# Last image of an attention and depthwise-conv kernel: division on chip for the last pair, four-part projection, x added by VectorE, and group averages on TensorE (first image too)

## The chip, the cores and the metric

The kernel runs on one core of a Trainium2 chip. Its time is device microseconds of one execution, the median of several. The engines are TensorE (PE in the profile; PEld is its weight load), VectorE (DVE), ScalarE (ACT), GpSimd (POOL) and SyncE (SP), which here only issues DMAs. Each engine takes its instructions in the order of the program and waits at the first one whose inputs or buffers are not ready. A DMA is issued from an engine's queue and waits there in the same way.

## The reference

x has shape (16, 384, 32, 32), all in fp32. Two layers, both with a residual and a group norm in front (32 groups of 12 channels):

```python
# _gn(v): (v - mean) / sqrt(var + 1e-5), per image, over a group's 12 channels and all pixels
def _L0_conv_ref(x, w_qkv, w_proj, b_proj):        # 8 heads of 48, n = 1024 pixels
    xt = x.reshape(b, c, n).transpose(0, 2, 1)
    qkv = einsum('bnc,oc->bno', xt, w_qkv)
    attn = softmax(einsum('bhnd,bhmd->bhnm', q, k) * SCALE)
    out = einsum('bhnm,bhmd->bhnd', attn, v)
    return einsum('bnc,oc->bno', out, w_proj) + b_proj
def _L1_conv_ref(x, weight):                       # depthwise, 7x7, padding 3
    w_sym = mean of the four rotations of weight
    return dwconv(x, w_sym)
x = x + _L0_conv_ref(_gn(x), ...)
x = x + _L1_conv_ref(_gn(x), weight)
```

## The kernel before

**Tiling.** An image is three tiles of 128 channels by 1024 pixels. The 8 heads are worked on in pairs, four pairs an image, 64 pairs in all (0 to 63); images are numbered 0 to 15. For a pair, attention runs over two halves of 512 queries and eight blocks of 128 keys. One step (`s_step`, `av_step`) is one half and one key block: two matmuls for the scores of the two heads, an exponential on ACT, two matmuls with v. Steps are issued in groups of four (GS), 16 groups an image; a group counts as r = 0, 4, 8 ... in the code, and is called group 0 to 15 here. V has a column of ones, so row 48 of a head's 64 accumulator rows holds the softmax sums. An fp32 matmul shows as two passes in the profile, each with its own weight load.

**Division and projection.** `take` copies a half of the accumulator to a tile `o` on ACT. `finish` then runs a chain: `sums_out` (L319, L320) writes the sum rows to DRAM and reads them back spread over partitions; `invert` takes the reciprocal (L326), writes it to DRAM (L328) and reads it back broadcast to 64 rows a head (L331); `divide` multiplies (L337). The fourth pair of an image is not projected by itself: its rows are copied by six DMAs (L342) into the unused rows of the three others, so that `proj_step` has three parts of 128 rows. `proj_step` ends with the bias on ACT (L360), and a DMA from POOL's queue that adds x in place (L361).

**Group norm.** `Stats.channels` takes channel statistics on VectorE (L184). `gather` sends them through DRAM so that one partition holds one group (L190, L192), `groups` aggregates them (L197), POOL works out scale and shift (L199 to L203), and two more DMAs through DRAM (L205, L209) bring them back to one row per channel. `apply` normalises a tile on a given engine (L215) or on ACT (L219).

**Depthwise conv.** For most tiles it is 49 multiply-adds on VectorE (`conv_tap`, L378), in place on the tile x1, and a DMA to the output from POOL's queue (L388). Of the last two images, tiles 2 and 1 go to TensorE instead: `conv_store` writes the normalised tile to DRAM (L450), `conv_load` reads shifted rows back (L457), four DMAs a load and two loads a half, `conv_on_pe` does a half of 16 rows with 112 passes (L478), and `conv_on_pe_end` adds the result from PSUM (L491). Its weight matrices are made by `conv_matrices` in group 4 and 6 of the last image.

**What sets the order.** The order on every engine is written out by a planner in the same Python code. `clock` stands for TensorE's time, `vclock` for VectorE's. After each group `catch_up` fills VectorE up to `clock`: a task of `later` whose due time has come, else the next conv tap of up to three active chains, each at an estimated cost (`us_tap`). `after(wait, cost, f)` sets a task due at `now() + wait`. The planner knows no lateness of the real engines: what it has put ahead of a task on VectorE stays ahead of it. After the last group a loop runs projection, conv halves (`half_on_pe`) and taps of the last two images until nothing is left. `check_vector` and `check_tensor` test all softmax sums for range at the end; a general version would run if they failed.

**Buffers.** PSUM has three two-bank tiles (`ps_s`, through `psum()`) for scores, q, k, v, projection and conv, and two one-bank tiles (`ps_o`) for attention. Tiles `o` have 6 buffers, x1 6, and `qk` 5, which the conv loads and one set of conv matrices share.

Of the kernel before, what the change touches and what calls it, by code (L numbers as in the profile page):

```python
# [10 lines left out]
F32 = mybir.dt.float32  # L11
# [10 lines left out]
SUM_LOW, SUM_HIGH = 1e-20, 1e20  # L22

# [17 lines left out]
def kernel(  # L41
# [7 lines left out]
    w_conv: bass.AP,  # L49
    out: bass.AP,  # L50
):

# [49 lines left out]
    def run(general):  # L102
        tag = "g" if general else "f"
        with ExitStack() as stack:
# [41 lines left out]
            load_x(0)  # L146
            wqk = wpool.tile([P, NK, 2, NK, P], F32, name="wqk")
# [11 lines left out]
            mhalf = wpool.tile([GROUPS, 1], F32, name="mhalf")  # L159
            nc.gpsimd.memset(mhalf, -0.5)  # L160
# [11 lines left out]
            wsh = wpool.tile([P, 2, 4, 2, KS], F32, name="wsh")  # L172

# [3 lines left out]
            class Stats:  # L177
# [16 lines left out]
                def groups(self):  # L194
# [6 lines left out]
                    nc.gpsimd.tensor_tensor(af[:, 0:1], ve, mhalf, ALU.pow)  # L201
# [8 lines left out]
                        self.sc, gr_d.rearrange("g e s -> (g e) s").rearrange("(k p) s -> p k s", p=P)  # L210
                    )
# [155 lines left out]

            def region(*ds):
                return [(slice(max(0, -d), H - max(0, d)), slice(max(0, d), H - max(0, -d))) for d in ds]
# [82 lines left out]
            def conv_load(b, k, h, a):  # L452
# [3 lines left out]
                for q in range(SH):  # L456
                    nc.sync.dma_start(  # L457
# [9 lines left out]
            def conv_on_pe(b, k, h):  # L467
                if h == 0:
                    pss[b, k] = psum(f"ps_conv_{b}_{k}")
# [4 lines left out]
                for n, (d0, dx) in enumerate(order):  # L474
                    _, (ox, ix) = region(0, dx)
# [115 lines left out]
            def us_tap(dy, dx):  # L591
                return ((H - abs(dy)) * (W - abs(dx)) + (130 if len(active) > 1 else 270)) / 940

            def tap():
# [3 lines left out]
                if not active:  # L598
                    return 0.0
                c = active.pop(0)  # L600
                b, k, n = c
                conv_tap(b, k, *TAPS[n])
                c[2] += 1
                took = us_tap(*TAPS[n])
# [40 lines left out]
            x1_made, lims = set(), []  # L645

            def project(b):
                nonlocal clock
                x1_made.add(b)
# [18 lines left out]
            def x1_chains(b, st):  # L668
                on_pe = [t for t in PE_TILES if t[0] == b]
                for k in range(NK - 1, -1, -1):  # L670
                    tail = b == B - 1
                    conv_begin(st, b, k, (nc.vector, nc.gpsimd, None)[k] if tail else nc.gpsimd)
                    if (b, k) in on_pe:
                        conv_store(b, k)
                        pe_conv.extend((b, k, h) for h in range(2))
                after(
                    1.0 if b == B - 1 else 6.0,
# [24 lines left out]
            def finish(u):  # L702
                sums_out(u)
                after(7.0, 0.3, lambda: finish2(u))
# [5 lines left out]
            def finish3(u):  # L710
# [4 lines left out]
                if u == U - 1:  # L715
                    after(0.5, 2.6, check_vector)
# [11 lines left out]
            st.gather()  # L728
            st.groups()
# [38 lines left out]
            def half_on_pe():  # L768
                nonlocal clock
                b, k, h = pe_conv.popleft()  # L770
                while (b, k, h, 1) not in shs:
                    loads(1)
                conv_on_pe(b, k, h)
# [91 lines left out]
```

## Time and profile before

| | |
|---|---|
| median of 3 runs | 3046.95 us (3046.26 to 3047.64) |
| the profiled execution's own time | 3048.38 us |
| its span, first to last instruction | 3046.5 us |
| TensorE clock granted, mean | 0.990 |
| DMA, mean over the span | 49 GB/s |

In a timeline, a row has the start in us, how long the row lasts (several instructions in a row are merged, "x36" counts them), the engine and the line, the operation, what it writes and reads, and in brackets the idle time of the engine before it with what ended it. "SPq" is a DMA that SP issues; the time is that of the issue. The start and the last 180 us are of interest here; the images between take 178 us each on TensorE.

How the share of busy time of the DMAs and TensorE's clock run in the tail, by stretches:

| us | PE busy | DVE busy | clock | DMA share, GB/s |
|---|---|---|---|---|
| 2840 to 2871 | 31.0 of 31 | 14.4 | 1.00 | 0.35, 101 |
| 2871 to 2881 | 2.1 of 10 | 9.7 | 0.82 | 0.90, 233 |
| 2881 to 2894 | 13.0 of 13 | 12.7 | 0.87 | 0.30, 71 |
| 2894 to 2921 | 0.4 of 27 | 26.4 | 0.57 | 0.23, 53 |
| 2921 to 2939 | 18.0 of 18 | 12.8 | 0.88 | 0.51, 96 |
| 2939 to 2973 | 34.0 of 34 | 5.3 | 1.00 | 0.55, 148 |
| 2973 to 3010 | 34.7 of 37 | 36.0 | 0.95 | 0.59, 149 |
| 3010 to 3046 | 13.9 of 36 | 24.9 | 0.75 | 0.08, 32 |

### The profile page before, as it was taken

Reading aid. Unit: us, or ns where it says so; the run is one execution under the profiler, and the core shown is the slowest. Engines: PE = TensorE matmul, PEld = TensorE weight load, DVE = VectorE, ACT = ScalarE, POOL = GpSimd, SP = SyncE. Lnnn points to the kernel's source line nnn. Section 1 sums busy time; section 2 is a strip of 40 time slices with the busy share of each in tenths; the row PEclk is TensorE's granted clock in tenths of the full one; section 3 lists DMA queues with packets and bytes.
Section 4 is the critical chain, followed back from the end, with each engine's and each line's share of the span. In section 5 each row is a group of like instructions: output and inputs, shape, how many; then the busy total and the mean of one; then the engine's idle time right before and its main releaser. Section 6 shows DMA issues by size and latency. Waiting matters only on the chain.

```text
span 3046.5 us, 30395 instructions
## 1 busy us (share of the span) xinstructions
PE 2955.0 (97%) x11586; PEld 1151.8 (38%) x11586; DVE 2606.9 (86%) x2532; ACT 1302.1 (43%) x1472; POOL 735.9 (24%) x440
## 2 busy tenths in 40 slices
PE   6999999999999999999999999999999999999866
PEld 2343343433434343343434334343433434343322
DVE  0001898996999999999999999999999999999757
ACT  1544435454443545434354543435354353535300
POOL 1021004020150604215060421506042150603310
PEclk9999999999999999999999999999999999999988
DMA  1113031021312112131211213121121312121343
GB/s 53 47 23 66 15 65 36 28 54 36 72 36 57 24 51 52 35 73 36 54 27 46 56 36 66 43 51 29 39 62 36 69 40 51 30 51 29 84 99 96
DMA packets 68252, 148.59 MB, mean 49 GB/s; under 512 B 31280, under 2 KB 33120, under 8 KB 66560
## 3 DMA queue, kind: packets, MB, share of 16 engines
q1 hardware_dynamic: 49280, 94.15, 12.6%
q0 software_dynamic: 18816, 52.40, 7.8%
q8 instruction: 93, 1.52, 0.2%
q14 instruction: 63, 0.52, 0.1%
HBM read 98.08 MB, written 29.54 MB: 42 GB/s over the span
## 4 chain that ended last, share of the span: by engine, by line
PE 93%; DVE 4%; issue 1%; DMA 1%; POOL 0%; SPq 0%; ACT 0%; POOLq 0%; DVEq 0%
PE ps_s L285 30%; PE acc L301 29%; PE ps_qk L234 17%; PE ps_proj L352 8%; PE ps_v L260 8%; DVE x L378 3%; PE ps_conv L478 1%; DMA x<-in_x 0%; DMA o<-o 0%; DMA wc<-in_w_conv 0%; POOL v L167 0%; DVE o L337 0%; DVE x L491 0%; DMA ch_x<-bs_x 0%; DMA sc_x<-gr_x 0%
## 5 line engine op out<-in xcount | busy, mean ns | idle before, releaser
L378 DVE SCALAR_TENSOR_TENSOR x<-xn,wsym,x 128x960 f32<-128x960 f32 (+9 forms) x2156 | 2382.0, 1175 | 19.0 <-POOL xn L215 15.8
L293 ACT ACTIVATE e<-ps_s 128x1024 f32<-128x1024 f32 x1024 | 967.1, 1030 | 394.4 <-PE ps_s L285 389.5
L285 PE MATMUL ps_s<-qk 48*128 48x512 f32 x4096 | 949.5, 603 | 2.2 <-ACT e L293 2.2
L301 PE MATMUL acc<-e,v 128*64 128x512 f32 x4096 | 937.7, 600 | 0.0
L285 PEld LDWEIGHTS ps_s<-qk 48*128 48x128 f32 x4096 | 373.3, 186 | 566.8 <-issue 430.6
L234 PE MATMUL ps_qk<-x,wqk 128*128 128x512 f32 x1152 | 507.6, 597 | 29.5 <-DVE x L215 29.5
L301 PEld LDWEIGHTS acc<-e,v 128*64 128x64 f32 x4096 | 272.0, 137 | 634.9 <-issue 563.2
L361 POOL DMA_DIRECT2D x<-in_x x48 | 42.3, 882 | 1488.1 <-ACT x L360 1483.1
L234 PEld LDWEIGHTS ps_qk<-x,wqk 128*128 128x128 f32 x1152 | 217.3, 191 | 312.5 <-issue 278.8
L199 POOL TENSOR_SCALAR ve_x<-mv_x 32x1 f32<-32x1 f32 x32 | 317.2, 9912 | 40.3 <-DVE mv_x L197 38.8
L241 ACT COPY qk<-ps_qk 128x1024 f32<-128x1024 f32 x96 | 97.2, 1012 | 465.6 <-PE ps_qk L234 465.6
L352 PE MATMUL ps_proj<-o,wp 128*128 128x512 f32 x576 | 253.6, 599 | 27.0 <-DMA o<-o 27.0
L260 PE MATMUL ps_v<-wv,x 128*128 128x384 f32 x768 | 254.5, 488 | 0.0
L184 DVE BATCH_NORM_STATS2 bs_x<-x 128x6 f32<-128x512 f32 x192 | 120.3, 681 | 109.6 <-DMA x<-in_x 92.2
L215 POOL TENSOR_SCALAR xn<-x,sc_x 128x1024 f32<-128x1024 f32 x46 | 195.1, 4248 | 40.1 <-DMA sc_x<-gr_x 40.0
L312 ACT COPY o<-acc 128x512 f32<-128x512 f32 x128 | 75.1, 587 | 296.7 <-PE acc L301 296.7
L260 PEld LDWEIGHTS ps_v<-wv,x 128*128 128x128 f32 x768 | 144.7, 190 | 113.6 <-issue 20.3
L326 DVE RECIPROCAL rec<-sums 128x16 f32<-128x16 f32 x64 | 16.0, 250 | 190.8 <-DMA sums<-sum 190.8
L352 PEld LDWEIGHTS ps_proj<-o,wp 128*128 128x128 f32 x576 | 109.0, 191 | 171.5 <-issue 167.9
L360 ACT ACTIVATE x<-ps_proj,bp 128x1024 f32<-128x1024 f32 x48 | 53.4, 1113 | 256.8 <-PE ps_proj L352 252.8
L269 ACT COPY v<-ps_v 128x384 f32<-128x384 f32 x128 | 55.1, 483 | 196.9 <-PE ps_v L260 196.9
L337 DVE TENSOR_TENSOR o<-o,inv 128x1024 f32<-128x1024 f32 x64 | 78.7, 1230 | 55.0 <-DMA inv<-inv 29.6
(48 smaller groups left out, 415.5 us busy)
## 6 DMA issues: line engine op xcount, KB each, us to landing
inv<-inv SPq DMA_DIRECT2D x128, 256.0 KB
x<-in_x SPq DMA_DIRECT2D x48, 512.0 KB
x<-in_x POOLq DMA_DIRECT2D x48, 512.0 KB, 5.5
out<-x POOLq DMA_DIRECT2D x48, 512.0 KB, 3.8
qk<-qk SPq DMA_DIRECT2D x96, 128.0 KB
sh<-xd SPq DMA_DIRECT2D x64, 160.0 KB
o<-o SPq DMA_DIRECT2D x96, 64.0 KB
sum<-o SPq DMA_DIRECT2D x128, 4.0 KB
```

The lines of the kernel that those rows point to most:

```text
L184: nc.vector.bn_stats(self.bs[:, k, 6 * h : 6 * h + 6], src[:, h * HALF : (h + 1) * HALF])
L199: nc.gpsimd.tensor_scalar(ve, mv[:, 1:2], EPS, None, ALU.add)
L215: engine.tensor_scalar(dst, src, self.sc[:, k, 0:1], self.sc[:, k, 1:2], ALU.mult, ALU.add)
L234: nc.tensor.matmul(ps[:, h, :], lhsT=wqk[:, k, s, t, :], rhs=xns[b][:, k, h * HALF : (h + 1) * HALF], start=(k == 0), stop=(k == NK - 1),)
L241: nc.scalar.copy(halves(qks[u][:, s, :]), ps)
L260: nc.tensor.matmul(ps[:, j, 0:C], lhsT=xns[b][:, k, t * P : (t + 1) * P], rhs=wv[:, k, :], start=(k == 0), stop=(k == NK - 1),)
L285: nc.tensor.matmul(ps[:, j, :], lhsT=qks[u][r, 1, i * P : (i + 1) * P], rhs=qks[u][r, 0, h * HALF : (h + 1) * HALF], start=True, stop=True,)
L293: nc.scalar.activation(es[n], ps, AF.Exp, scale=SCALE)
L301: nc.tensor.matmul(accs[u, h][64 * j : 64 * j + 64, :], lhsT=v_of(u, i, j), rhs=e[:, j, :], start=(i == 0), stop=(i == NT - 1),)
L337: nc.vector.tensor_tensor(os_[u], os_[u], invs.pop(u), ALU.mult)
L352: nc.tensor.matmul(ps[:, h, :], lhsT=wp[:, t, o * P : (o + 1) * P], rhs=os_[NP * b + t][:, h * HALF : (h + 1) * HALF], start=(t == 0), sto ...
L378: nc.vector.scalar_tensor_tensor(acc, xn1s[b, k].rearrange("p (h w) -> p h w", w=W)[:, iy, ix], wsym[:, k, dy + PAD, dx + PAD : dx + PAD + 1],
```

## The change

Two inputs come from the host: `masks`, seven 128x128 blocks that average over a group's 12 channels (the three diagonal blocks and the four neighbours that share a group) and an eighth block that copies a head's sum row to its 64 rows; and `w_proj_4`, projection weights in four parts, one for each pair as it lies in its `o` tile, with zero rows for the rest.

In the first image the group statistics no longer go through DRAM. In the last image the last pair is divided half by half: a mask matmul spreads the sums, VectorE takes the reciprocal of 128x512 from PSUM and multiplies. The projection has four parts and is split: parts 0 and 1 are issued ahead of the last attention half's last four v steps, parts 2 and 3 after them. x is loaded straight into the x1 tiles, and VectorE adds projection, bias and x. A conv half on TensorE is cut in two pieces of 56 passes; conv loads in the tail are issued from SP and ACT in turn; the engines that normalise the last image's three tiles change; and the planner charges 0.06 us more for a tap of the last two images.

```diff
+            masks_0 = opool.tile([P, N], F32, tag="o", name="masks_0")
+                nc.sync.dma_start(masks_0, masks.rearrange("p b c -> p (b c)"))
...
+                def groups_on_pe(self, masks):
+                    st = small.tile([P, NK, 2], F32, tag="st", name=f"st_{self.name}")
+                    for k in range(NK):
+                        nc.vector.bn_aggr(st[:, k, :], self.bs[:, k, :])
+                    ps = ps_o.tile([P, HALF], F32, tag="acc", name=f"ps_st_{self.name}")
+                    def average(c0, src):
+                        for mo in range(NK):
+                            blocks = [n for n, b in enumerate(MASK_BLOCKS) if b[1] == mo]
+                            for n in blocks:
+                                ki = MASK_BLOCKS[n][0]
+                                nc.tensor.matmul(
+                                    ps[:, c0 + mo : c0 + mo + 1],
+                                    lhsT=masks[:, n, :],
+                                    rhs=src[:, ki : ki + 1],
...
+                    nc.vector.tensor_copy(mean, st[:, :, 0])
+                    average(0, mean)
+                    nc.vector.tensor_tensor(d, mean, ps[:, 0:NK], ALU.subtract)
+                    nc.vector.tensor_tensor(d, d, d, ALU.mult)
+                    nc.vector.tensor_tensor(d, d, st[:, :, 1], ALU.add)
+                    average(NK, d)
+                    nc.vector.tensor_scalar(d, ps[:, NK : 2 * NK], EPS, None, ALU.add)
+                    nc.gpsimd.tensor_tensor(self.sc[:, :, 0], d, mhalf, ALU.pow)
+                    nc.vector.scalar_tensor_tensor(
+                        self.sc[:, :, 1], ps[:, 0:NK], -1.0, self.sc[:, :, 0], ALU.mult, ALU.mult
...
+            def divide_at_once(u, h):
+                half = os_[u][:, h * HALF : (h + 1) * HALF]
+                ps = ps_o.tile([P, HALF], F32, tag="acc", name=f"ps_sum_{u}_{h}")
+                nc.tensor.matmul(ps, lhsT=late["masks"][:, 7, :], rhs=half, start=True, stop=True)
+                inv = tpool.tile([P, N], F32, tag="t", name=f"inv_{u}_{h}")[:, 0:HALF]
+                nc.vector.reciprocal(inv, ps)
+                nc.vector.tensor_tensor(half, half, inv, ALU.mult)
...
+            def proj_part(b, o, ts):
+                if o not in pps:
+                    pps[o] = psum(f"ps_proj_{b}_{o}")
...
+            def residual(b, o):
+                nc.vector.scalar_tensor_tensor(
+                    halves(x1s[b, o]), pps.pop(o), bp[:, o : o + 1], halves(x1s[b, o]), ALU.add, ALU.add
...
-                    nc.sync.dma_start(
+                    (nc.scalar if late.get("tail") and q % 2 else nc.sync).dma_start(
...
-                return ((H - abs(dy)) * (W - abs(dx)) + (130 if len(active) > 1 else 270)) / 940
+                late_us = 0.06 if active[0][0] >= B - 2 else 0.0
+                return ((H - abs(dy)) * (W - abs(dx)) + (130 if len(active) > 1 else 270)) / 940 + late_us
...
-                    conv_begin(st, b, k, (nc.vector, nc.gpsimd, None)[k] if tail else nc.gpsimd)
+                    conv_begin(st, b, k, (nc.gpsimd, None, nc.vector)[k] if tail else nc.gpsimd)
...
-                after(7.0, 0.3, lambda: finish2(u))
+                if u < U - 1:
+                    after(7.0, 0.3, lambda: finish2(u))
...
-            st.gather()
-            st.groups()
+            st.groups_on_pe(masks_0.rearrange("p (b c) -> p b c", c=P))
...
+                if n0 == NS - 2 * GS:
+                    after(3.5, 4.2, lambda: None)
+                    divide_at_once(U - 1, 0)
+                if n0 == NS - GS:
+                    for o in range(NK):
+                        proj_part(B - 1, o, (0, 1))
+                    clock += 2 * US_PROJ
...
+                    if r == 8 * GS:
+                        w4 = w_proj_4.rearrange("(t p) c -> p t c", p=P)
+                        nc.sync.dma_start(wp, w4[:, 0:NK])
+                        nc.sync.dma_start(late["w3"], w4[:, NK])
...
+                    if r == 8 * GS:
+                        t = opool.tile([P, N], F32, tag="o", name="masks_1")
+                        nc.sync.dma_start(t, masks.rearrange("p b c -> p (b c)"))
+                    if r >= 9 * GS and (b, 0) not in x1s and all(c[0] > b - 2 for c in active):
+                        for k in range(NK):
+                            x1s[b, k] = rpool.tile([P, N], F32, tag="x1", name=f"x1_{b}_{k}")
+                            nc.gpsimd.dma_start(
+                                x1s[b, k], x[b, k * P : (k + 1) * P].rearrange("p h w -> p (h w)")
...
-            while later or proj or chains or active or pe_conv:
-                if proj and proj[0][0] <= clock + 1.0:
-                    project(proj.popleft()[1])
-                elif pe_conv and (B - 1 in x1_made or pe_conv[0][2] == 0):
+            late["tail"] = True
+            b = B - 1
+            divide_at_once(U - 1, 1)
+            for t in (NP - 2, NP - 1):
+                for o in range(NK):
+                    proj_part(b, o, (t,))
+            clock += US_PROJ * 4 / 3 + 1.0
+            st = Stats(f"x1_{b}")
+            for o in range(NK):
+                residual(b, o)
+                st.channels(x1s[b, o], o)
+            conv_piece()
+            st.groups_on_pe(late["masks"])
+            clock += 7.0
+            x1_chains(b, st)
+            vclock = clock
+            after(4.0, 2.6, check_vector)
+            while later or chains or active or pe_conv:
+                if pe_conv:
...
-                    half_on_pe()
+                    conv_piece()
```

`conv_piece` is `half_on_pe` for one of two parts of a half: seven of the fourteen shifts, four row groups each. `x1_chains` is called without waiting for the six DMAs and POOL's steps that `gather` and `groups` made.

## The prediction

> **What bounds the kernel now.** I read the page first, then the chain of waits, then the timelines of single engines at both ends of the span. Image numbers run from 0 to 15, pairs of heads from 0 to 63, so image 15 owns pairs 60 to 63.
>
> ```profile
> PE 2955.0 (97%) x11586; PEld 1151.8 (38%) x11586; DVE 2606.9 (86%) x2532; ACT 1302.1 (43%) x1472; POOL 735.9 (24%) x440
> PE 93%; DVE 4%; issue 1%; DMA 1%; POOL 0%; SPq 0%; ACT 0%; POOLq 0%; DVEq 0%
> ```
>
> TensorE is busy for 2955.0 of 3046.5 us, which leaves 91.5 us idle. The timelines place nearly all of it: 29.46 before the first matmul, 7.87 + 26.60 + 2.4 after the last attention step, 22.6 after the last matmul; that is 88.9. So the middle is closed to this change, and what it can give lies at the two ends.
>
> The head, from the timeline:
>
> ```profile
> 8.03 3.65 DVE L184 BATCH_NORM_STATS2 bs_x<-x 128x6 f32<-128x512 f32 x6
> 14.23 0.78 POOL L190 DMA_DIRECT2D ch_x<-bs_x  x1
> 19.18 0.79 DVE L197 BATCH_NORM_AGGREGATE mv_x<-gs_x 32x2 f32<-32x144 f32 x1 [7.50 <-DMA gs_x<-ch_x]
> 28.59 0.81 DVE L215 TENSOR_SCALAR x<-x,sc_x 128x1024 f32<-128x1024 f32 x1 [8.61 <-DMA sc_x<-gr_x]
> 29.46 23.20 PE L234 MATMUL ps_qk<-x,wqk 128*128 128x512 f32 x48 [29.46 <-DVE x L215]
> ```
>
> The channel statistics are done at 11.68, yet x is normalised at 28.59: the 17 us between are four small DMAs in a row and POOL's memsets ahead of them.
>
> The tail, TensorE:
>
> ```profile
> 2868.24 3.65 PE L301 MATMUL acc<-e,v 128*64 128x512 f32 x16
> ...
> 2880.74 13.36 PE L478 MATMUL ps_conv<-sh,mat 128*32 128x512 f32 x108 [7.87 <-DMA sh<-xd]
> 2920.71 17.95 PE L352 MATMUL ps_proj<-o,wp 128*128 128x512 f32 x36 [26.60 <-DMA o<-o]
> 2938.59 34.37 PE L478 MATMUL ps_conv<-sh,mat 128*32 128x512 f32 x336
> ```
>
> and VectorE, whose last tap ends the kernel (3027.47 + 8.14 = 3035.61; one output DMA and the end of the program take the other 10.9):
>
> ```profile
> 2856.55 1.23 DVE L337 TENSOR_TENSOR o<-o,inv 128x1024 f32<-128x1024 f32 x1 [19.22 <-issue]
> 2857.69 11.60 DVE L378 SCALAR_TENSOR_TENSOR x<-xn,wsym,x 128x928 f32<-128x928 f32 x11
> 2869.20 0.25 DVE L326 RECIPROCAL rec<-sums 128x16 f32<-128x16 f32 x1
> 2869.37 15.43 DVE L378 SCALAR_TENSOR_TENSOR x<-xn,wsym,x 128x1024 f32<-128x1024 f32 x13
> 2884.71 1.22 DVE L337 TENSOR_TENSOR o<-o,inv 128x1024 f32<-128x1024 f32 x1
> ...
> 2896.71 0.25 DVE L326 RECIPROCAL rec<-sums 128x16 f32<-128x16 f32 x1
> 2896.87 19.65 DVE L378 SCALAR_TENSOR_TENSOR x<-xn,wsym,x 128x928 f32<-128x928 f32 x16
> 2916.43 1.22 DVE L337 TENSOR_TENSOR o<-o,inv 128x1024 f32<-128x1024 f32 x1
> ...
> 2964.20 0.82 DVE L215 TENSOR_SCALAR xn<-x,sc_x 128x1024 f32<-128x1024 f32 x1 [12.00 <-DMA sc_x<-gr_x]
> 2973.10 0.15 DVE L756 TENSOR_REDUCE good<-ps_again 1x1 f32<-1x2 f32 x1 [8.08 <-PE ps_again L754]
> ```
>
> The three divides are those of pairs 61, 62 and 63. Pair 63's attention ended at 2871.9 but was divided at 2916.43, because its reciprocal and its multiply each stood behind conv taps in VectorE's strict order. VectorE runs late, by the planner's clock some 25 us: pair 62's reciprocal is due about when group 11 ends (2843) and ran at 2869.20. The cause:
>
> ```profile
> 2799.00 38.42 POOL L199 TENSOR_SCALAR ve_x<-mv_x 32x1 f32<-32x1 f32 x1 [12.98 <-DVE mv_x L197]
> 2847.26 1.50 SPq L450 DMA_DIRECT2D xd<-xn  x2
> 2848.81 0.45 SPq L328 DMA_DIRECT2D inv<-rec  x1
> ```
>
> POOL's tiny operation (0.23 us in an idle stretch) is held until the taps stop at 2837.33; SP's store of image 14 waits for POOL; pair 61's inverse waits behind that store; VectorE stands 19.22 us for it. The change touches none of this, so the lateness stays, and it decides how much of the tail can be won. VectorE's idle time from 2856.55 to 3035.61 is 2.62 + 3.67 + 3.75 + 3.51 + 12.00 + 8.08 = 33.6 us, its work 145.4.
>
> **The change, part by part** (times on the old trace's clock).
>
> *Head.* Four DMAs and a [32]-row aggregation go. Added: a 512 KB load ahead of wqk on SP, three aggregations, a copy, two rounds of 7 fp32 matmuls (14 passes each, with one weight load per pass), three small VectorE operations between the rounds, one after, POOL's power, one VectorE operation. Steps: 11.7 end of statistics; 0.5 for the wc load sharing the DMAs (x moved at 400 GB/s, so 512 KB is 1.3 us, the upper end); aggregation 0.79 for 144 elements against 0.15 for a one-element operation gives 0.2 each, 0.6; copy 0.15; first round 14 x 0.34 (the weight load of a cold start) = 4.8; three operations 0.7 with hand-overs; second round 3.8 (between 14 x 0.34 and the warm 14 x 0.19); 0.25; POOL 0.57 + 0.2 (its memsets end at 14.3, before this); 0.25. Sum 23.5 against 28.59: 5.1 won. In the old head the first six passes run at 0.86 instead of 0.43, 2.5 us; some of it may be gone after the small matmuls: 0.4. **Taken: 5.5.** One-column passes are not in the trace: by ps_again's two (0.19 together) the 28 cost 2.7 and the gain would be 11, where wqk's landing stops it (the DMAs fall silent at about 16.5); by full 512-column warm passes (0.43) they cost 12 and it is 1.
>
> *Weights and masks on SP in group 8.* Three more DMAs, 1.3 MB, issued behind the blocked store, from 2852.5. At the 194 GB/s of that stretch 6.8 us, at the head's 400 GB/s 3.3, and about 1.5 to issue: masks are there at 2857 to 2861, and the first mask matmul is due at 2861.05. Queued behind them on SP are the conv loads of groups 10, 12 and 14 and pair 62's sums, needed at 2869.2 and before landed early enough. Taken: nothing; if the cover is gone each us stops TensorE, which has 20 us before VectorE reaches that half.
>
> *Loop end on TensorE.* One mask matmul 0.87 and 12 projection matmuls at 0.87 (a step's six take 5.2) before the last attention half: attention ends at 2883.2 instead of 2871.9. Projection over four pairs is 24 matmuls, 20.8 us instead of 15.65.
>
> *VectorE's queue.* From pair 61's divide (2856.55): 11 taps and pair 62's reciprocal to 2869.4, as before; 11 taps to 2882.6; first half's reciprocal and multiply; 2 taps and pair 62's divide to 2890.5; by the planner 13 more taps (the last group is 10.6 longer), to 2906; then the second half's reciprocal and multiply, to 2910.4. A 128x512 reciprocal is not in the trace. From 128x16 at 0.25 against 0.15 for one element: 6.7 ns an element, 3.6 + 0.15, **3.7 us taken**; lower end a 512-element statistics pass, 0.64; upper 32 x 0.25 = 8.0. Multiply 0.62.
>
> The Trainium skill ("VectorE: DVE Perf Modes", First, the fixed hardware budget) says that Reciprocal is an iterative divide with a repeat count of 8. At the 0.96 GHz of its Specifications, an estimate of 8 cycles for each of 512 elements is 4.3 us; the sum would end 1.2 us later.
>
> So pair 63 is divided 7 us earlier than before, not 40: its DRAM round trip goes, the taps ahead of it stay. TensorE does t=2 after 2890.5, idles to 2910.4, and runs t=3 in 7.7 (six passes at 0.86, six at 0.43).
>
> *Residual.* ACT's bias and POOL's accumulating DMA (1.11 + 5.5 landing) give way to 3 VectorE operations of 1.22 from PSUM. x is loaded early, after image 13's stores at 2870; 1.5 MB beside 1.3 MB of conv loads at 230 GB/s lands by 2887, needed at 2914. The statistics end at 2922. The first conv piece (56 passes, 5.7) stands ahead of the averages on TensorE until 2924; the averages then take two rounds of 3.5 plus 2 of small operations: 2933, against 2964.20 before.
>
> *Sum for VectorE.* Work: 145.4 - 0.25 - 1.14 - 0.79 + 2 x 4.32 + 3 x 1.22 + 1.5 (small ones) = 157.0. Taps: image 15's chain alone took 59.1 for 49 (1.206); three chains together 30 in 31.9 (1.063). 46 taps now run as two chains; the gain is 0 to 6.6, 5 taken: 152.0. Idle: 3.9 (for t=3), 9.5 (averages), 2 (POOL normalises tile 0 in 1.73, held while taps run, released when VectorE waits for it), 2 (check), 1: 18.4. End 2856.55 + 152.0 + 18.4 = 3027.0 against 3035.6: **8.6 won**.
>
> *Conv on TensorE* covers little now: 15 pieces at 5.8 from 2931.7, one wait of about 6 for loads queued behind the two stores of image 15, gives 3025 against 3023.9 before; VectorE's add after it ends level with the taps. Loads issued on ACT too: 302 to 1581 ns an issue before, so at most 0.5 us a load off SP; taken at nothing, ACT has one normalisation left.
>
> The Trainium skill ("DMA: Bandwidth & Descriptors", Issuing engines are not separate DMA queues) speaks against more: a second issuing engine saves issue time only. With the stretches at 1.05 share and 227 to 233 GB/s here, that would leave the 6 us wait whole.
>
> **Total** 5.5 + 8.6 = 14.1. The profiled span, 3046.5, is 0.45 below the shown median (its own run took 3048.38), so 3046.95 - 14.1 = **3033**.
>
> **Rivals.** *TensorE's conv becomes the bound* (chance 0.20). Before, one conv half ran in the wait for pair 63; now PSUM is held by the projection and all eight run after it. At 6.0 a piece (444 passes in 47.48) and two waits of 5 more the end is 3034: tail 1.5 won, **3040**. For it: 7.87 and 1.84 us waits for conv loads; against: loads run at 230 GB/s, 5.7 us a half, where TensorE takes 11.4. *Late VectorE recovers* (0.12): no stall at 19.22 with the shifted order, head at its good end: 9 + 15, **3023**. *Slower* (0.06): the same conv loads as a lasting bound. If each half waits 3 us and more for its rows, as DMAs from two queues and outputs meet, the seven halves after the first give 21 us: 3053; it decides from 2.0 us a half on, and the DMA share of 0.55 to 0.59 there is against it. *No effect* (0.03): masks late in the head, averages as slow as the DMAs, about 3046. The forecast has 0.59.
>
> The forecast alone spans 3027 to 3039; with the others and both ends of the unknown costs, 3022 to 3043. A measurement tells about 0.2% (6 us) from no change: faster by more 0.90, within 0.04, slower 0.06.
>
> **What would show it.** Right: first qk matmul near 24; a 128x512 reciprocal near 3.7; the second one starting 20 us or more after attention ends; projection t=3 waiting on that multiply; a gap of some 9 us on VectorE at the averages; last tap and last conv add within 3 us of each other. Wrong: TensorE waiting at the mask matmul; conv matmuls waiting for rows at most pieces; a last-half reciprocal with no taps ahead.

## The result, and the profile after

| | before | after |
|---|---|---|
| median of 4 runs, us | 3046.61 (3045.91 to 3047.64) | 3022.47 (3021.12 to 3024.64) |
| span of the profiled execution, us | 3046.5 | 3020.0 |
| TensorE clock granted, mean | 0.990 | 0.994 |

The change made the kernel faster: ratio 0.9921, 95% interval 0.9904 to 0.9938, 24.1 us in the medians. The forecast was 14.1 us and 3033, with a range of 3022 to 3043: the sign is right, the gain is 10 us larger than forecast, and the time lies 0.5 us inside the range. The forecast's own span, 3027 to 3039, misses it by 4.5 us.

The page of after, busy times and the shares of the chain of waits:

```profile
PE 2970.3 (98%) x11658; PEld 1166.2 (39%) x11658; DVE 2616.1 (87%) x2553; ACT 1298.7 (43%) x1469; POOL 728.3 (24%) x426
PE 90%; DVE 5%; issue 3%; POOL 1%; DMA 1%; ACT 0%; POOLq 0%; SPq 0%; DVEq 0%
```

TensorE has 15 us more to do (a fourth projection part, the mask matmuls) and idles 49.7 us instead of 91.5. So the gain, but for a place in the loop shown below, is idle time of TensorE at the two ends, and for the tail it is VectorE that decides how much.

*Head*, timeline of TensorE:

```profile
14.41 3.15 PE L236 MATMUL ps_st_x<-mn_x,masks 128*128 128x1 f32 x14 [14.41 <-DVE mn_x L245]
18.20 3.15 PE L236 MATMUL ps_st_x<-d_x,masks 128*128 128x1 f32 x14 [0.64 <-DVE d_x L250]
23.69 6.50 PE L280 MATMUL ps_qk<-x,wqk 128*128 128x512 f32 x11 [2.34 <-DVE x L261]
```

The first qk matmul stands at 23.69 instead of 29.46. Each round of 14 one-column passes takes 3.15 us, 0.225 a pass. Of the qk passes that follow four take the long 0.86 instead of six, so after image 0's first qk the kernel is 6.6 us ahead. In before, image 0's projection also waits 0.37 us for a row copy; in after it doesn't, and from there the kernel is 7.0 us ahead. The profile's clock shows 1.00 for all these rows, yet the long passes take as long as those at 0.50 in the tail (0.86), and so do the rounds (3.14 us at 0.50 in run e8, 1.72 at 1.00). That TensorE ran at half clock here is worked out from these times; the clock's row doesn't show it.

*A place in the loop that the change doesn't touch.* In group 10 of image 2 TensorE waits 2.22 us for an exponential, in both kernels. Before:

```profile
512.28 2.08 PE L285 MATMUL ps_s<-qk 48*128 48x512 f32 x4 [2.22 <-ACT e L293]
514.29 5.91 PE L301 MATMUL acc<-e,v 128*64 128x512 f32 x16
```

and after:

```profile
505.29 1.13 PE L331 MATMUL ps_s<-qk 48*128 48x512 f32 x4 [2.22 <-ACT e L339]
506.35 3.65 PE L347 MATMUL acc<-e,v 128*64 128x512 f32 x16
```

The same 20 passes take 7.92 us before and 4.71 after: in the profiled execution of before the granted clock fell to 0.50 there, in that of after it stayed at 1.00. That is 3.2 of the 26.5 us between the two spans. It is no effect of the change, as the twelve further traces show below.

*Tail*, VectorE:

```profile
2846.16 1.22 DVE L383 TENSOR_TENSOR o<-o,inv 128x1024 f32<-128x1024 f32 x1 [18.85 <-ACT e L339]
...
2894.01 3.35 DVE L420 RECIPROCAL inv<-ps_sum 128x512 f32<-128x512 f32 x1
2897.46 0.69 DVE L421 TENSOR_TENSOR o<-o,inv 128x512 f32<-128x512 f32 x1
2900.32 1.28 DVE L440 SCALAR_TENSOR_TENSOR x<-ps_proj,bp,x 128x1024 f32<-128x1024 f32 x1 [2.17 <-PE ps_proj L431]
...
2913.33 0.16 DVE L248 TENSOR_TENSOR d_x<-mn_x,ps_st_x 128x3 f32<-128x3 f32 x1 [4.03 <-PE ps_st_x L236]
...
3008.17 1.22 DVE L570 TENSOR_TENSOR x<-ps_conv,x 128x1024 f32<-128x1024 f32 x1
```

and TensorE:

```profile
2898.20 7.53 PE L431 MATMUL ps_proj<-o,mat 128*128 128x512 f32 x10 [10.94 <-DVE o L421]
2905.66 5.98 PE L557 MATMUL ps_conv<-sh,mat 128*32 128x512 f32 x56
2911.57 1.72 PE L236 MATMUL ps_st_x<-mn_x,masks 128*128 128x1 f32 x14
2913.94 2.71 PE L236 MATMUL ps_st_x<-d_x,masks 128*128 128x1 f32 x14 [0.65 <-DVE d_x L250]
2916.58 42.51 PE L557 MATMUL ps_conv<-sh,mat 128*32 128x464 f32 x388
```

Pair 61's divide (the first line) still stands 18.85 us, as it did before (19.22). From its start to VectorE's last instruction it is 163.2 us (2846.16 to 3009.39), before 179.1: **15.8 us won in the tail**. The named waits in that stretch are 2.17 and 0.81 for the projection's fourth part, 4.03, 2.80 and 1.01 in the averages, 10.8 together, against 33.6 before. TensorE runs its conv from 2916.58 to 3005.48 without once waiting for a row. Its clock fell to 0.50 once more during the second round of averages (2.71 us for 14 passes where the first took 1.72) and was back at 1.00 by 2922; no wait since 2898.20 had been longer than 0.65 us. That is about 1 us of VectorE's 2.80.

So 7.0 (head) + 3.2 (clock) + 15.8 (tail) + 0.5 (the rest) make the 26.5 us between the spans.

### The profile page after: what moved, and what is told of

The parts are those of the page before. It is cut to its first block, busy times and chain, and to the rows that moved or that the text cites. A ratio compares the mean times of both kernels' runs of the same rounds, so it can differ in the third digit from the quotient of the medians.

```text
span 3020.0 us, 30559 instructions
## 1 busy us (share of the span) xinstructions
PE 2970.3 (98%) x11658; PEld 1166.2 (39%) x11658; DVE 2616.1 (87%) x2553; ACT 1298.7 (43%) x1469; POOL 728.3 (24%) x426
## 4 chain that ended last, share of the span: by engine, by line
PE 90%; DVE 5%; issue 3%; POOL 1%; DMA 1%; ACT 0%; POOLq 0%; SPq 0%; DVEq 0%
PE ps_s L331 29%; PE acc L347 29%; PE ps_qk L280 16%; PE ps_v L306 8%; PE ps_proj L398 8%; DVE x L455 4%; POOL ve_x L210 1%; DMA wc<-in_w_conv 0%; PE ps_st_x L236 0%; DVE bs_x L195 0%; DMA out<-x 0%; DVE x L570 0%; DMA sums<-sum 0%; DMA sum<-o 0%; DVE o L383 0%
## 5 line engine op out<-in xcount | busy, mean ns | idle before, releaser
L398 PE MATMUL ps_proj<-o,wp 128*128 128x512 f32 x540 | 235.7, 595 | 0.2 <-DVE bs_x L195 0.2
L372 DVE RECIPROCAL rec<-sums 128x16 f32<-128x16 f32 x63 | 15.8, 250 | 185.4 <-DMA sums<-sum 185.3
L398 PEld LDWEIGHTS ps_proj<-o,wp 128*128 128x128 f32 x540 | 101.4, 190 | 134.4 <-issue 131.4
```

The costliest lines, as they stand in the source:

```text
L398: nc.tensor.matmul(ps[:, h, :], lhsT=wp[:, t, o * P : (o + 1) * P], rhs=os_[NP * b + t][:, h * HALF : (h + 1) * HALF], start=(t == 0), sto ...
```

## The experiments

**The theories.** A: the head is worth a fixed 7 us; in the tail VectorE's stretch from pair 61's divide to its end decides the time, so each wait put into it or taken out of it shows in the end; the loop's 3 us are chance. Against it stand, by the part: that the parts are worth something else alone (B), and that TensorE's conv takes over as the bound (B or C, as each text says). No kernel here leaves out any of the computation. Twelve kernels ran in three sets beside the kernel before, whose median was 3046.99 in the set of e1 to e4, 3046.86 in that of e5 to e8 and 3045.84 in that of e9 to e12. The kernel after ran in none of them: a median set against its 3022.47 comes from another set. The stretch of VectorE (from pair 61's divide to its last instruction, 163.2 us in after) doesn't hang on the loop's place, which alone differs by 3.3 us between profiled executions. So a difference of some 3 us from after in the medians is not resolved, and the stretch, of one execution each, is given beside it.

| run | what differs | median, us | ratio to before, 95% |
|---|---|---|---|
| e1_head | before + new head | 3040.34 | 0.9978 (0.9969 to 0.9987) |
| e2_tail | after, old head | 3031.00 | 0.9944 (0.9931 to 0.9958) |
| e3_dram | after, last pair divided through DRAM | 3024.68 | 0.9930 (0.9916 to 0.9943) |
| e4_avg_dram | after, last averages through DRAM | 3033.97 | 0.9956 (0.9943 to 0.9970) |
| e9_fold | after, old three-part projection | 3036.74 | 0.9968 (0.9956 to 0.9981) |
| e10_resid | after, x added by ACT and a DMA | 3030.67 | 0.9950 (0.9933 to 0.9967) |
| e11_sp | after, tail's conv loads on SP alone | 3024.09 | 0.9926 (0.9910 to 0.9943) |
| e5_order | after, 13 taps moved behind the division | 3020.86 | 0.9915 (0.9902 to 0.9929) |
| e6_fill | after, six taps put into gaps | 3020.77 | 0.9916 (0.9903 to 0.9930) |
| e7_release | after, POOL released by VectorE | **3007.54** | 0.9872 (0.9857 to 0.9887) |
| e8_release_fill | e7 + e6 | **3005.90** | 0.9865 (0.9850 to 0.9880) |
| e12_rel_ord_fill | e7 + e6 + e5 | 3009.09 | 0.9877 (0.9861 to 0.9894) |

### Head alone, tail alone

e1_head is the kernel before with `groups_on_pe` and its masks in the first image and nothing else; e2_tail is the kernel after with the head undone:

```diff
-            masks_0 = opool.tile([P, N], F32, tag="o", name="masks_0")
-            if not general:
-                nc.sync.dma_start(masks_0, masks.rearrange("p b c -> p (b c)"))
...
-            st.groups_on_pe(masks_0.rearrange("p (b c) -> p b c", c=P))
+            st.gather()
+            st.groups()
```

> The kernel before with one part of the change: the first image's group averages on TensorE (masks loaded ahead of wqk). The profile of the changed kernel has its first qk matmul at 23.69 instead of 29.46 and reaches the third image's qk 7.0 us earlier; another 3.2 us appear at 514 us, where the old trace shows TensorE at half clock after a 2.22 us wait and the new one shows the same wait at full clock. Theory A (the head is a fixed 7 us, the 3.2 us are chance in when the clock drops): 3039 to 3040, 7 us below the kernel before, and the place at 514 us may look either way. Theory B (an earlier start is all eaten later by VectorE's late queue in the tail, because only VectorE's end counts): under 2 us gained. Theory C (the head brings the whole 10.4 us by which the changed kernel's pair 61 is early): 3036.

> The changed kernel with the first image's averages back through DRAM, so the tail's part of the change alone. From pair 61's divide to VectorE's last instruction the old trace takes 179.1 us and the new one 163.2. Theory A (head and tail add up): 3030 to 3031, about 16 us below the kernel before, and 163 us again between these two points. Theory B (my prediction's size for the tail, 8.6): 3038. Theory C (part of the tail's gain hangs on the earlier start): the stretch differs from 163 by more than 3 us.

The head alone brought 6.7 us (3046.99 to 3040.34), with its first qk matmul at 23.53; the tail alone 16.0, its VectorE stretch 163.2 us as in the kernel after. 6.7 + 16.0 = 22.7, against 24.1 for both. Head and tail add up to within 1.4 us, less than the loop's place varies by itself: its 16 passes with v took 5.72 us in e1 and 5.05 in e2, where after has 3.65. So A holds in both (e1 lies 0.3 above its 3040), and the rivals fall: the head is not eaten up in the tail, the tail brings more than 8.6, and its stretch doesn't hang on the earlier start.

### The parts of the tail, undone one at a time

e3 divides the whole last pair through DRAM, at the second half's place in VectorE's order:

```diff
-                    after(3.5, 4.2, lambda: None)
-                    divide_at_once(U - 1, 0)
+                    pass
...
-            divide_at_once(U - 1, 1)
+            invert(U - 1)
+            nc.vector.tensor_tensor(os_[U - 1], os_[U - 1], invs.pop(U - 1), ALU.mult)
```

> The changed kernel with the last pair divided through DRAM again (sums already read back, one reciprocal of 128x16, write, broadcast, one multiply of 128x1024), but at the same place in VectorE's order, after the loop; projection with its own weights stays. Theory A (what held pair 63 back was the taps ahead of it on VectorE, not the DRAM trip): VectorE gives up 2 x (3.35 + 0.69) = 8.1 us of work, gets 1.4 back and waits about 4.6 for two DMAs, so the time is that of the changed kernel within 3 us, 3020 to 3025, with projection of the fourth part starting about 2 us later. Theory B (the DRAM trip is the gain): 6 us or more lost, over 3028.

VectorE's multiply now waits for the inverse; its timeline:

```profile
2903.77 1.23 DVE L925 TENSOR_TENSOR o<-o,inv 128x1024 f32<-128x1024 f32 x1 [6.20 <-DMA inv<-inv]
```

Its stretch is 162.5 us, 0.7 shorter than after, though 1 us of that is the clock in the second round of averages (1.72 us here, 2.71 in after); the median is 2.2 higher, in a kernel whose profiled execution has the loop's slow place (5.91 us). It is in A's range. The part that the change is named for first is worth 2 us at most, which these runs don't resolve: it takes a wait of 6.2 us off VectorE and gives it two reciprocals of 3.35 us, 6.7 together. The 44 us that pair 63 lay undivided before were taps planned ahead of it, not the trip.

e4 takes the last image's averages back to DRAM and POOL (`gather` and `groups` in place of `groups_on_pe(late["masks"])`).

> The changed kernel with the last image's group averages through DRAM and POOL again; the first image keeps TensorE's. From the last channel statistics to the normalisation the old way took 17.4 us (2946.8 to 2964.2) and the new way 9.3 (2908.8 to 2918.1). Theory A (VectorE's sum of work and waits sets the end): 7 to 8 us lost, 3030. Theory B (TensorE's conv sets the end): TensorE is relieved of 4.4 us of averages and does conv pieces instead, so no loss, 3019 to 3023.

The longest of the new waits on VectorE:

```profile
2926.44 0.81 DVE L261 TENSOR_SCALAR xn<-x,sc_x 128x1024 f32<-128x1024 f32 x1 [8.36 <-DMA sc_x<-gr_x]
```

With 4.54 us for the gathered statistics before it and 4.86 at the check behind it, the stretch is 172.85 us, 9.6 longer, and the median 11.5 higher. The stores of the normalised tiles are later too, so TensorE now waits 14.26 us for its conv rows, and the check, which needs TensorE, makes VectorE wait. B (no loss) falls; A has the way but too small a size (7 to 8 us): the 4.86 at the check is not in it.

e9 undoes the fourth pair's own weights: the six row copies come back, and three parts are projected, all after the division.

```diff
-                            stop=(t == NP - 1),
+                            stop=(t == NK - 1),
...
-                    for o in range(NK):
-                        proj_part(B - 1, o, (0, 1))
                     clock += 2 * US_PROJ
...
-                        nc.sync.dma_start(wp, w4[:, 0:NK])
...
-            for t in (NP - 2, NP - 1):
-                for o in range(NK):
-                    proj_part(b, o, (t,))
+            for t in range(NK):
+                for j in range(2):
+                    r = 64 * j
+                    nc.sync.dma_start(
+                        os_[NP * b + t][r + D : r + 64, :],
+                        os_[U - 1][r + 16 * t : r + 16 * t + 16, :],
+                    )
+            for o in range(NK):
+                proj_part(b, o, range(NK))
```

> The kernel after, but the fourth pair is projected as before: six DMAs copy its rows into the other three tiles after the division, and then three parts are projected, none of them ahead of the last attention half. Theory A (VectorE's stretch from pair 61's divide decides, so a wait put into it costs its length): the second multiply ends at 2898.2, the copies take 3.1 (as before, 2917.65 to 2920.71), TensorE then needs 7.7 for the first step at the cold clock and 5.2 for each of the others, so the third addition of x starts near 2919.3 instead of 2906: 13 us more, 3035.5 (3031 to 3038). Theory B (the split of the projection and the own weights are hidden by the wait for VectorE's reciprocal and change nothing): 3021 to 3025.

```profile
2912.64 1.28 DVE L440 SCALAR_TENSOR_TENSOR x<-ps_proj,bp,x 128x1024 f32<-128x1024 f32 x1 [10.16 <-PE ps_proj L431]
```

That wait on VectorE and two of 2.55 us after it stand where after has 2.17 and 0.81. The stretch is 175.05 us, 11.8 longer; the median is 14.3 higher. A, in its range: of the parts undone here, this one carries most. It is two things at once, the copies and the order (nothing projected ahead of the last attention half), and no run tells them apart.

e10 takes the addition of x back to ACT (bias) and POOL's accumulating DMA, and leaves out the early load of x.

> The kernel after, but bias by ACT and x by a DMA that accumulates from POOL's queue, as before, in place of VectorE's three operations and the early load of x. Theory A: 1.1 for ACT and 5.5 for the DMA stand between the third projection step and its statistics in place of 1.25 of VectorE: statistics 5 us later, 3027.5 (3025 to 3030). Theory B (the DMA hides behind the other tiles' steps and VectorE saves 3.8 us of work): 3018 to 3023.

```profile
2910.48 1.29 DVE L195 BATCH_NORM_STATS2 bs_x<-x 128x6 f32<-128x512 f32 x2 [8.88 <-DMA x<-in_x]
```

With 2.89 and 0.61 for the other tiles VectorE waits 12.4 us for the DMAs, in place of 3.0 for the projection and 3.8 of its own work. The stretch is 167.76 us, 4.5 longer, as A has it; the median is 8.2 higher, 3.7 more than the stretch, and 0.7 above A's range. The profiled execution lost 3.3 us against that of after at the loop's slow place; whether the medians differ for the same reason no run shows.

The four undone parts cost 2.2, 11.5, 14.3 and 8.2 in medians, 36 together, and -0.7, 9.6, 11.8 and 4.5 in stretches, 25 together, where the whole tail brings 16. So they don't add. One reading is that the planner's new order has taken away the taps that ran during the old waits, so that a part undone by itself costs more than it brought; no run shows it. No run takes back the conv's finer pieces, the engines of the three normalisations or the planner's 0.06 us a tap.

e11 issues the tail's conv loads from SP alone.

> The kernel after, but all conv loads in the tail are issued from SP alone. Theory A (issue time is no limit, VectorE's taps end last): no change, 3020.5 to 3024.5. Theory B (the second issuing queue is what kept TensorE's conv from waiting for its rows, the 6 us that the prediction put there): TensorE waits for rows at several pieces, the last addition waits for it, 3026 or more.

3024.09, 1.6 above after, in A's range; the stretch is 164.3 us, 1.0 longer. TensorE waits for rows once, 1.00 us, and VectorE 0.78 at the check. But e6, which issues from both queues, waits 1.12 us at the same place: no gain from the second queue is shown that stands out from what these kernels vary by.

### The order of VectorE's work

e5 lets the planner put no taps into the last group, so that the 13 that stood ahead of the second half's reciprocal come later:

```diff
                 clock += GS * US_STEP + US_TURN
+                if n0 == NS - GS:
+                    vclock = max(vclock, clock)
```

> The changed kernel with the 13 taps of the last attention group planned after the last pair's division instead of ahead of it; no work is added or taken. In the changed kernel TensorE stands 10.9 us for the second half's multiply while VectorE works those taps. Theory A (VectorE's sum of work and waits sets the end, TensorE's wait is covered): the second reciprocal starts some 16 us earlier, TensorE's wait goes and its conv ends 10 to 15 us earlier, but VectorE now waits for projection about 3 us more; 3022 to 3027, no gain. Theory B (the late division is on the path, as the wait on TensorE suggests): 8 to 11 us gained, 3011 to 3014.

```profile
2880.54 3.35 DVE L420 RECIPROCAL inv<-ps_sum 128x512 f32<-128x512 f32 x1
...
2888.44 1.28 DVE L440 SCALAR_TENSOR_TENSOR x<-ps_proj,bp,x 128x1024 f32<-128x1024 f32 x1 [3.77 <-PE ps_proj L431]
```

The reciprocal starts at 2880.54 instead of 2894.01 and TensorE's wait of 10.94 us is gone; its conv ends near 2991, 14 us earlier. The median gains 1.6 us; VectorE's stretch is 159.2, 4.0 shorter. Its waits hardly change (9.9 us for 10.8: 3.77 for 2.17 and 0.81 at the projection, 6.12 for 7.84 in the averages); 2.3 us are busy time, in taps that ran in another order, and the rest are small gaps. VectorE is the bound, so A's mechanism holds, though the time is 1.1 us below A's range, and B (8 to 11 us from TensorE's wait) falls: the most striking wait in TensorE's timeline was worth next to nothing.

e6 puts taps where VectorE waits (one ahead of the additions, three and two in the averages):

```diff
                     average(0, mean)
+                    for _ in range(3 if self.name == f"x1_{B - 1}" else 0):
+                        tap()
...
                     average(NK, d)
+                    for _ in range(2 if self.name == f"x1_{B - 1}" else 0):
+                        tap()
...
             st = Stats(f"x1_{b}")
+            for _ in range(1):
+                tap()
```

> The changed kernel with six conv taps of image 14 moved into VectorE's gaps of the last image's residual and group averages: one ahead of the first residual, three behind the first round of averages, two behind the second. The gaps were 2.17 + 0.81, 4.03 and 2.80 us. Theory A (VectorE sets the end, with TensorE's conv close behind: its last pass ends at 3005.3 and VectorE's last add starts at 3008.2): the gaps shrink by some 6 us, the gain is cut at 2 to 3, 3019 to 3021. Theory B (nothing but VectorE counts): 5 to 6 gained, 3016 to 3018. Theory C (the gaps are no loss, because taps in them only delay the normalisation that the last chain waits for): no gain or up to 2 lost.

```profile
3006.54 1.23 DVE L574 TENSOR_TENSOR x<-ps_conv,x 128x1024 f32<-128x1024 f32 x1 [3.31 <-PE ps_conv L561]
```

The stretch is 4.4 us shorter (158.8), and would be 7.7 shorter but for this line: the last addition now waits 3.31 us for TensorE's conv. The median, 3020.77, is 1.7 below after and in A's range; B (3016 to 3018) falls. In after the conv ends 2.7 us before the last addition starts: by no more than that is VectorE the bound over TensorE.

### The late VectorE

e7 removes what the prediction called the cause of VectorE's lateness, a POOL operation held while taps run. A copy by VectorE of POOL's result makes VectorE itself wait, and image 14's three tiles are normalised by VectorE instead of POOL:

```diff
+                    self.af = af
...
                 st.groups()
+                if b == B - 2:
+                    seen = small.tile([GROUPS, 2], F32, tag="seen", name="seen")
+                    nc.vector.tensor_copy(seen, st.af)
...
-                    conv_begin(st, b, k, (nc.gpsimd, None, nc.vector)[k] if tail else nc.gpsimd)
+                    conv_begin(st, b, k, (nc.gpsimd, None, nc.vector)[k] if tail else nc.vector if b == B - 2 else nc.gpsimd)
```

> The changed kernel with the cause of VectorE's lateness taken away: in image 14's group norm VectorE copies POOL's result right after its aggregation, so that it stands still for about 2 us and POOL's four small operations run instead of being held for 38.4 us under the taps; and image 14's three tiles are normalised by VectorE (3 x 0.82) instead of POOL. Theory A (the held POOL operation, through SP's store of the normalised tile and pair 61's inverse queued behind it, makes VectorE's 18.9 us stand at pair 61's divide, and VectorE's end is the kernel's end): the stand shrinks to under 5, 10 to 14 us gained net of 4.5 us of new work and waits, 3008 to 3012. Theory B (the stand has another cause, a late DMA of its own): no gain, 3021 to 3027. Theory C (TensorE's conv takes over as the bound at once): 3 to 6 gained.

From the timelines of POOL and SP in after:

```profile
2788.99 38.41 POOL L210 TENSOR_SCALAR ve_x<-mv_x 32x1 f32<-32x1 f32 x1 [12.72 <-DVE mv_x L208]
2836.68 1.51 SPq L527 DMA_DIRECT2D xd<-xn  x2
2838.24 0.45 SPq L374 DMA_DIRECT2D inv<-rec  x1
```

and of POOL, VectorE and SP in e7:

```profile
2792.64 0.23 POOL L210 TENSOR_SCALAR ve_x<-mv_x 32x1 f32<-32x1 f32 x1 [12.95 <-DVE mv_x L208]
...
2794.16 0.16 DVE L748 COPY seen<-af_x 32x2 f32<-32x2 f32 x1 [1.61 <-POOL af_x L214]
...
2812.32 1.04 SPq L528 DMA_DIRECT2D xd<-xn  x2
...
2834.90 1.21 DVE L384 TENSOR_TENSOR o<-o,inv 128x1024 f32<-128x1024 f32 x1
```

The same operation lasted 38.41 us in the kernel after. Here it lasts 0.23, for 1.61 us of waiting on VectorE; SP's store follows at 2812.32 instead of 2836.68, pair 61's divide comes at 2834.90 with no stand before it, and TensorE waits 2.03 us for the fourth part instead of 10.94. The kernel takes 3007.54 us, 14.9 below after and 39 below before, 0.5 below A's range. Pair 61's divide comes 11.3 us earlier, and the stretch behind it is 3.0 us shorter (160.2). This shows the cause: POOL held by the taps, SP's queue held by POOL, VectorE held by SP. The run makes two edits, the copy and the three normalisations taken off POOL; how much of the gain each brings no run shows.

The Trainium skill ("SBUF — State Buffer", Who interferes with whom) says that a VectorE instruction with two SBUF inputs contends with a GpSimd instruction that reads SBUF. A tap has two such inputs, and the rows agree: 38.41 us beside taps, 0.23 us while VectorE waits. Earlier images show it too: in after POOL's same operation is held for 18.93 us from 467.98, 21.29 from 826.47, 20.54 from 1004.14 and 20.55 from 1183.50, each time until VectorE next waits.

e8 adds e6's six taps to e7, e12 adds e5's order as well.

> Both of the edits before together: POOL released and image 14 normalised by VectorE, and six taps moved into the gaps of the last image's averages. Theory A (VectorE's sum): the gains add up as long as TensorE's conv ends earlier too, which it does when the division comes earlier; 3003 to 3008. Theory C (TensorE's conv is the bound by then): no better than the release alone, 3008 to 3012.

> The release of POOL (e7), the six taps in the gaps (e6) and the 13 taps behind the division (e5) together. In e8 the last addition waited 3.4 for TensorE's conv. Theory A (VectorE is the bound once TensorE is let go earlier): TensorE's conv ends some 8 us earlier, the wait goes, 3002.5 (3000 to 3005). Theory C (what TensorE wins is lost again on VectorE, which now stands for the projection 2 to 4 us with no taps planned there): 3005 to 3009.

e8 takes 3005.90, 1.6 below e7 (the intervals overlap), and its last addition waits 3.38 us for TensorE's conv. It is in A's range, and the conv cuts the gain as in e6. e12 was meant to take that wait away and is slower:

```profile
2878.49 3.36 DVE L425 RECIPROCAL inv<-ps_sum 128x512 f32<-128x512 f32 x1 [11.05 <-PE ps_sum L423]
```

TensorE's conv ends at 2988.3 and VectorE at 2998.4, so VectorE is the bound again, as A said; but it stands 11.05 us for the end of attention, where in e5 it was late anyway. A's time falls; C's time is missed by 0.1 us, and the stand is not the one that C priced at 2 to 4 us (that one is 1.66). The median is 3.2 above e8 (the intervals overlap), the stretch 164.1 us, 5.4 longer than e8's 158.75. So the order with the taps ahead costs 4.0 us of stretch with VectorE 19 us late (after against e5) and saves 5.4 with VectorE on time (e8 against e12).

## Why the prediction was right, and where its sizes were off

**Head (5.5 forecast, 7.0 in the trace, 6.7 alone).** Mechanism right, first qk forecast near 24, at 23.69. Of the pieces, the copy took 1.79 us instead of 0.15, beside a memset of POOL's (8.78 to 14.33), and the first round 3.15 instead of 4.8, which cancel: that is luck. The 1.5 us too little have three parts. The steps won 5.77 instead of 5.1, for which the second round (3.15 instead of 3.8) is enough; the shorter qk passes won 0.8 instead of 0.4; and the wait for a row copy at image 0's projection, 0.4, was not in the sum. The low end of the gain was also added up wrongly: 28 passes at 0.43 leave 5.1 - 3.4 + 0.4, about 2, and not 1.

**Tail (8.6 forecast, 15.8 in the trace, 16.0 alone).** The term that failed is "Idle: ... 18.4". VectorE's work, reckoned like the forecast's 152.0 as the stretch less its named waits, is 163.2 - 10.8 = 152.4. The idle term by its own parts: for t=3 3.0 instead of 3.9; the averages 7.8 instead of 9.5; POOL's hold, the check and "1" (5 together) no wait. POOL's normalisation of tile 0 started at 2918.13, beside VectorE's own, and was done at 2920.94, amid taps: it was not held, and cost VectorE only a tap of 1.87 us where the taps around it take 1.2 to 1.3. 30 taps stood between the check's start and its last step, so it waited for nobody. 18.4 - 10.8 = 7.6 is the whole error of the tail, less 0.4 of work. Both halves of the reciprocal took 3.35, forecast 3.7; the forecast's own row, 6.7 ns for each of 512 elements and 0.15, makes 3.6. The second started 20.6 us after TensorE's last attention pass (2873.4), as forecast.

The forecast's reading of the Trainium skill ("VectorE: DVE Perf Modes", First, the fixed hardware budget) as 8 cycles an element had given an estimate of 4.3 us; the measurement, 3.35, is below it, and below the forecast's row too.

**Clock (not in the forecast).** 3.2 us of the difference between the two spans. In traces of kernels that differ from after only in the last two images, the same 16 passes took 3.65 (e5), 4.40 to 4.95 (e7, e8, e11, e12) and 5.72 to 6.03 us (e3, e4, e6, e9, e10), always behind a wait of 2.22. Up to there the ten issue the same instructions, so no edit sets it.

**What was said to cost nothing.** The masks on SP: one weight load waited 0.76 us for them, behind running matmuls; in e5 and e6 TensorE itself waited, 0.31 and 0.24 us. One sign of being wrong did show in another way: TensorE waited 1.90 us at the second half's mask matmul, but for VectorE's first reciprocal, and that wait lies ahead of the 10.94 that e5 shows to be worth next to nothing. The conv loads: "one wait of about 6" did not come; conv ends at 3005.5, 15 pieces at 5.93, and the last addition starts 2.7 us after. The lateness of VectorE "stays": 18.85 against 19.22.

**The rivals.** "TensorE's conv becomes the bound" (3040) did not happen, though it was 2.7 us away in after, and in e6 and e8 the last addition waits 3.3 us for the conv. "Late VectorE recovers" (3023) has the measured time but not its mechanism, so its time is luck: the stand is still there. Its price of 6 us more was far too low as well: e7 removes the stand and gains 14.9. The slower case would have needed TensorE to wait 2 us a half for rows; it waited 0.

The forecast got the limit right (VectorE's order in the tail), and e5 bears it out. That the time is still inside the range is partly luck: the lower end, 3022, was opened by the rival of a recovered VectorE and by the ends of the unknown costs, neither of which came true as told; what came true is an idle term 7.6 us smaller. The forecast gave no price for each part of the tail, and so did not see that the division on chip, undone alone, changes next to nothing (e3).

## What to carry to other kernels

A wait that a timeline shows on one engine (10.94 us on TensorE) was worth next to nothing while another engine's stretch of work and waits was the longer; add up that stretch before moving anything. The parts of this change didn't add when each was undone against the new order: a fixed order of instructions fits one lateness, and with the lateness gone the same order can lose (e5 against e12). An operation that lasts a hundred times its length beside another engine's work can be a cheaper thing to mend than the chain of waits behind it: a dependent copy, with three normalisations moved, was worth 15 us.

## What the runs showed of the hardware

- POOL's small operation was not let in between VectorE's taps: 38.41 us instead of 0.23, until VectorE stopped; a VectorE instruction that needs POOL's result ended that within 1.61 us. A POOL normalisation that had started beside one of VectorE's (2918.13) did end amid taps, in 2.81 us instead of 1.73.
- After a wait of 2.22 us TensorE's clock sometimes fell to 0.50 and sometimes didn't: 16 passes in 3.65 to 6.03 us, by the execution. The Trainium skill ("TensorE: Matmul & The Clock Gate", Part 1, What's actually happening) gives an idle window of about 3.4 us for the slow clock, and says of the way back to the fast one that it varies from run to run. The rows show the fall itself to vary, and behind a shorter wait.
- The clock also fell while TensorE worked on one-column passes: to 0.50 near 2914.5 in after, in the second of two rounds of 14, with a wait of 0.65 us between them. In e3, e6 and e9 both rounds took 1.72 us at 1.00 or near it.
- A matmul pass of one column with its own weights took 0.225 us in the head (3.15 for 14) and 0.123 in the tail at a clock of 1.00 (1.72 for 14); at 0.50 a round took 3.14 (e8).
- The reciprocal of 128x512 from PSUM took 3.35 us, 6.7 for a pair's two halves; the division of the same pair through DRAM made VectorE wait 6.20. The two kernels' stretches differ by 0.7 us.
